# The first block of experts is laid over the attention's early tiles, and token slots carry their row's mean and inverse deviation

## The chip, the cores and the metric

The kernel runs on one core of a Trainium2 chip. Its time is the device time of one execution in microseconds (us), the median of three runs where not said otherwise. The core has five engines with queues of their own: TensorE (PE in the profile; its weight loads are shown apart as PEld), VectorE (DVE), ScalarE (ACT), GpSimd (POOL) and SyncE (SP, which here only issues DMAs). Each works through its queue in order and waits at an instruction until its semaphores are there. Sixteen DMA engines move data for all of them.

## The reference

A tensor `x` of 4 images, 32 by 32 tokens, 384 channels, float32, goes through two layers:

```
x = x + L0_conv(ln(x))      # attention of 12 heads, 1024 tokens an image, with a grouped top-96 mask
t = t + L0_ffn(ln(t))       # 4 experts, the best 2 for each token, 384 -> 1536 -> 384 with gelu
x = x + L1_conv(ln(x))      # outlook attention over 3 by 3 windows
t = t + L1_ffn(ln(t))       # feed-forward whose weights are Kronecker products
```

The part that matters here is the second line. For each token, `ln` takes the mean and the variance of its 384 channels and gives `(v - m) / sqrt(s + 1e-5)`. A gate (384 to 4, then softmax) chooses two experts and their shares; each chosen expert computes `gelu(v @ w1 + b1) @ w2 + b2`; the two answers are added with their shares. The gate needs the same mean and deviation as the experts do.

## The kernel before

**Stages.** `attention` (line 139) runs first, then `experts` (1452), then `outlook` (1596) and `Kron.run` (1936). At the very end stands a general attention behind a run-time test, which these inputs do not enter. On PE, DVE, ACT and SP the instructions of `attention` and `experts` stand in the order in which the Python code issues them. POOL's queue is different: there a planner, which estimates when each instruction will be ready, sets the order when the kernel is built. So a POOL instruction of `experts` can stand among those of `attention`.

**The attention.** There are 48 heads (12 for each image) and four steps a head (`PAIRS`), each with two tiles of 128 keys by 1024 queries. In a step PE makes scores (line 596), ACT the exponentials `e` (606), PE their sums over keys (`total`, 614 into `ps_z`). Once a head has its sums, four small DMAs turn them and spread their reciprocals over the partitions: `z_row` and `zz` (`gather`, 630 and 632), `r_row` and `rz` (`spread`, 644 and 646), all issued by SP. Six steps behind the scores DVE multiplies `e` by `rz` (`share`, 652), and a step later PE multiplies by the values (`out`, 614 into `ps_o`). At the end of a head `keep` copies `ps_o` to the one buffer `po` (672) and adds it up in `q`, by two SP DMAs (681) and two accumulating POOL DMAs (679).

Beside the heads run the preparation of the next image (projections with `wqkv`, transposes into `xnT`, groups with `g`, `gpbd`, `qmbd`), the search for the top 96 (`topk`), the output projection of the image before (`project`), and its routing (`routed`, then `Router.route`), one step of each at a time.

**The routing.** `project` takes the statistics of each finished row with `bn_stats` and `bn_aggr` (722, 723) into `im["mv"]`; `routed` makes the inverse deviation `rs` (742, 752) and the logits; `route` chooses the experts and gives every token two slots in a table in DRAM, of 64 bytes each (`LINE` = 16 words). All 16 words hold the token's number: POOL fills `ids` with an `iota` (1313) and writes it with 16 indirect DMAs (1317), which wait for the slot numbers `there` from DVE (1306). When image 2 of 0 to 3 is routed, `Router.first` (1325) works out the experts and rows of the first four blocks (`NFIRST`), the last of it being `rows_w_first` and `rows_t_first` (1383). Image 3 is routed inside `experts`.

**The end of the attention.** After the last head, DVE and PE make a check over `zall`, `onehot` and `topped` (lines 873 to 887) that sets the flag of the run-time test.

**The experts.** There are 35 blocks of 256 slots. For block n POOL loads by indirect DMA the expert's weights `up` (128 by 4620, 2.37 MB) and `down` (128 by 4992, 2.56 MB; both line 1479), the slots' token numbers `ids` (1490) and the 256 rows of `x1` into `xb` (two DMAs, 1500). `norm` makes the rows' statistics and normalises `xb` in place:

```
nc.vector.bn_stats(st, xb[:, t, :])                                    # 1511, two times
nc.vector.bn_aggr(mv[:, t, :], st)                                     # 1512, two times
nc.scalar.activation(rs, mv[:, :, 1], AF.Sqrt, bias=net.eps["t"])      # 1513
nc.vector.reciprocal(rs, rs)                                           # 1514
nc.vector.tensor_scalar(xb[:, t, :], xb[:, t, :], mv[:, t, 0:1], ...)  # 1516, two times
```

`turn` transposes it into `xbT` (1526, copies 1527). Then PE makes 12 groups of three matmuls into `ps_h` (1568), each followed by a gelu on ACT (1572), and two rows of 12 into `ps_y` (1583), to which DVE adds the bias (1588) and which SP stores (1589). `norm(n + 1)` is issued after the gelus of block n and `turn(n + 1)` before the last row of `ps_y`. Between the gelus of blocks 0 and 1, `beside` puts the projection of image 3 (eight times line 265) and its routing and schedule.

**Memory.** A stage's pools lie on a stack in SBUF and are given back when the stage ends; a tile of the next stage lies where tiles of the last one lay, and its first write waits until those it covers were read for the last time (`reuse_waits="tile"`). Attention and experts begin at the same address. Bytes per partition, from the shapes: `at_const` begins with `wqkv` 13,872, `gpbd` 2,304, `hsel`, `qmbd` 2,304 and holds the check's `topped`, `zall`, `onehot`; `at_big` has `xt` 6,144, `g` 10,240, `xnT` 12,288, three `k` of 4,096, `q4`, `k4`, and `v` 12,288. Over them lie `ex_w1` (two `up` of 18,480), `ex_w2` (two `down` of 19,968), and `ex_blk` (six `ids` of 128, two `xb` and two `xbT` of 3,072). So the first `up` lies over `wqkv`, `gpbd`, `hsel` and most of `qmbd`; the first `down` over the end of `g`, over `xnT` and over two of the `k`; `ids` and `xb` over `v`.

Of the kernel before, what the change touches and what calls it, by code (L numbers as in the profile page):

```python
# [10 lines left out]
FP = mybir.dt.float32  # L11
AF = mybir.ActivationFunctionType
ALU = mybir.AluOpType
# [125 lines left out]
def attention(net, outer, router, x, x1, unsafe, qkv_wT, gpT, proj_wT, proj_w, gate_w, gate_b):  # L139
# [23 lines left out]
    psum = router.psum  # L163
    with ExitStack() as ctx:
        const = ctx.enter_context(tc.tile_pool(name="at_const", bufs=1))
        big = ctx.enter_context(tc.tile_pool(name="at_big", bufs=1))
# [11 lines left out]
        def fetch(b, half, tag="xt"):  # L178
            xt = xts[b, half] = big.tile([P, 4, C], FP, name="xt", tag=tag)
            r = b * NTOK + 512 * half  # L180
            nc.sync.dma_start(out=xt, in_=x[r : r + 512, :].rearrange("(t p) c -> p t c", p=P))

        fetch(0, 0)
        fetch(0, 1, "g")
        wqkv = const.tile([P, KC, 3 * C + NE], FP, name="wqkv")
        for part in range(3):
# [8 lines left out]

        gpbd = const.tile([P, KC, GW], FP, name="gpbd")
        nc.gpsimd.memset(gpbd, 0.0)
# [12 lines left out]
        for t in range(5):  # L210
            for n in range(4):
# [9 lines left out]
                )  # L221
        qmbd = const.tile([P, KC, GW], FP, name="qmbd")
        nc.gpsimd.memset(qmbd, 0.0)
# [17 lines left out]
        def gating():  # L241

            by = big.tile([P, KC, C], FP, name="proj", tag="xt")
            nc.scalar.dma_start(out=by, in_=proj_w.rearrange("(k p) i -> p k i", p=P))
# [181 lines left out]
        def prepare(b):  # L426
# [5 lines left out]
            yield 0, lambda: b == 0 or b - 1 in valued  # L432
            xnT = im["xnT"] = big.tile([P, KC, NTOK], FP, name="xnT", tag="xnT")
            for name in ("col", "inv"):
# [68 lines left out]
        def groups(b):  # L503

            im = images[b]
            for c in range(KC):
                yield 0, lambda: (b, c, "qk") in reached
                q = im["q"][c]

                g = big.tile([P, NB, P + GW], FP, name="g", tag="g")  # L510
                for half in range(2):
# [218 lines left out]
        def routed(b):  # L730
# [23 lines left out]
            nc.vector.tensor_tensor(logit, logit, gate(bgate), ALU.add)  # L754
            yield from router.route(b, logit)
            if b == B - 2:
# [413 lines left out]
class Router:  # L1170
# [67 lines left out]

    def route(self, b, logit):

# [71 lines left out]
        ids = self.temp("ids", [P, NB, self.LINE], mybir.dt.int32)  # L1312
        nc.gpsimd.iota(ids, pattern=[[P, NB], [0, self.LINE]], base=b * NTOK, channel_multiplier=1)
        sent = []
        for t in range(NB):
# [136 lines left out]
def experts(net, router, x1, x2, wup, wdown, beside):  # L1452
# [10 lines left out]
    with ExitStack() as ctx:  # L1463
        def pool(name, bufs, **kw):
            return ctx.enter_context(tc.tile_pool(name=name, bufs=bufs, reuse_waits="tile", **kw))

        wp1, wp2 = pool("ex_w1", 2), pool("ex_w2", 2)
        blk, hp, work = pool("ex_blk", 2), pool("ex_h", 14), pool("ex_work", 4)
        ps_h, ps_y = pool("ex_ps_h", 3, space=PSUM), pool("ex_ps_y", 3, space=PSUM)
# [5 lines left out]
        def weights(n):  # L1475
            up = wp1.tile([P, KC * HID + NF], FP, name="up", tag="up")
            down = wp2.tile([P, NF * C + C], FP, name="down", tag="down")
            for t, w in ((up, wup), (down, wdown)):
                nc.gpsimd.indirect_dma_start(
                    out=t, out_offset=None, in_=w,  # L1480
                    in_offset=bass.IndirectOffsetOnAxis(ap=rows(n)[0], axis=0),
                )
            return up, down
# [4 lines left out]
        def tokens(n):  # L1488
            t = ids[n] = blk.tile([P, TT, router.LINE], I32, name="ids", tag="ids", bufs=6)
            nc.gpsimd.indirect_dma_start(  # L1490
                out=t.rearrange("p t w -> p (t w)"), out_offset=None,
                in_=net.table.rearrange("(r t) w -> r (t w)", t=TT),
                in_offset=bass.IndirectOffsetOnAxis(ap=rows(n)[1], axis=0),
            )

        def fetch(n):
            xb = xbs[n] = blk.tile([P, TT, C], FP, name="xb", tag="xb")
            last = (B - 1 if n < NFIRST else B) * NTOK
# [6 lines left out]
        def norm(n):  # L1505
            xb = xbs[n]
            mv = work.tile([P, TT, 2], FP, name="ln_mv", tag="ln_mv")
            rs = work.tile([P, TT], FP, name="ln_rs", tag="ln_rs")
            for t in range(TT):
                st = work.tile([P, 6], FP, name="ln_st", tag="ln_st")  # L1510
                nc.vector.bn_stats(st, xb[:, t, :])
                nc.vector.bn_aggr(mv[:, t, :], st)
            nc.scalar.activation(rs, mv[:, :, 1], AF.Sqrt, bias=net.eps["t"])  # L1513
            nc.vector.reciprocal(rs, rs)  # L1514
            for t in range(TT):
                nc.vector.tensor_scalar(
                    xb[:, t, :], xb[:, t, :], mv[:, t, 0:1], rs[:, t : t + 1], ALU.subtract, ALU.mult
                )

        def turn(n):  # L1520
            xb = xbs.pop(n)
            xbT = blk.tile([P, KC, XB], FP, name="xbT", tag="xbT")
            for t in range(TT):
# [497 lines left out]
def gates(net, psum, gate_w, gate_b):  # L2021

    tc, nc = net.tc, net.nc
    with ExitStack() as ctx:
# [6 lines left out]
        for b in range(B):  # L2031
            mv, rs = net.ln_stats(range(b * NB, (b + 1) * NB), "t")
            logit = work.tile([P, NB, NE], FP, name="logit", tag="logit")
            for t in range(NB):
# [12 lines left out]
                nc.vector.tensor_tensor(logit[:, t, :], ps[:, :NE], bgate, ALU.add)  # L2047
            yield logit


@with_exitstack
def metaformer_kernel(
# [70 lines left out]
    with tc.If(tc.nc.values_load(unsafe[0:1, 0:1], min_val=0, max_val=1) != 0):  # L2123
        with ExitStack() as outer:
# [4 lines left out]
            with ExitStack() as inner:  # L2129
                router = routing(inner)  # L2130
                for b, logit in enumerate(gates(net, router.psum, gate_w, gate_b)):
                    for _ in router.route(b, logit):
                        pass
# [63 lines left out]
```

## Time and profile before

| what | us |
|---|---|
| median of three runs | 3019.83 (3013.11 to 3023.88) |
| the profiled execution | 3045.37 |
| its span in the profile | 3043.6 |
| attention, to the end of the last `ps_o` matmuls | 0 to 1295.3 |
| from there to block 0's first `ps_h` matmul | 1295.3 to 1321.4 |
| blocks 0 and 1 with projection and routing of image 3 | 1321.4 to 1420.4 |
| blocks 2 to 34 | 1420.4 to 2467.4 |
| outlook and last feed-forward | 2467.4 to 3043.6 |

All but the first row are of one profiled execution, whose own time is 25.5 us above the median of the runs. In the profile's page, part 1 has the busy time of each engine, part 2 the span in 40 slices of 76 us (each digit the busy share in tenths), part 4 the chain of work that ended last, part 5 the groups of like instructions. A line of a group reads: line, engine, operation, output and inputs, shapes, count, then busy time and mean time of one, then how long the engine sat idle before them and what ended it. In answers about a stretch of time, each row begins with the start and the duration in us.

### The profile page before, as it was taken

The page shows a single profiled execution, that of the slowest core. Times are in us where ns is not written, and L with a number is a line of the kernel's source. Part 1 is how long each engine was busy: PE and PEld are TensorE (multiplying, and loading weights), DVE is VectorE, ACT ScalarE, POOL GpSimd, SP SyncE. Part 2 cuts the span into 40 slices and gives each one's busy share as a digit, 9 for nine tenths or more (in the row PEclk, how much of TensorE's full clock was granted, in tenths as well). Part 3 has the DMA queues.
Part 4 walks back from the last instruction along what each step waited for, and adds up shares of the span by engine and source line. Part 5 has one row for each costly group of instructions (what it writes and reads, how often), then busy time and mean ns, then how long its engine had stood idle before and what let it go on. Part 6 is the DMA issues. An engine that isn't in the chain of part 4 may idle for free.

```text
span 3043.6 us, 36874 instructions
## 1 busy us (share of the span) xinstructions
PE 2792.6 (92%) x13236; PEld 1505.7 (49%) x13236; DVE 1398.5 (46%) x3871; ACT 1316.2 (43%) x2130; POOL 390.6 (13%) x496
## 2 busy tenths in 40 slices
PE   6979998899889986668999999999999978999998
PEld 3323343333333431145777777777777744444443
DVE  1467667666766676624111111111111137767652
ACT  3677777677767765312222222222222222212125
POOL 1000000200020002123111112221211012000000
PEclk9999999999999998879999999999999989999999
DMA  5133334222322231254445545555555456544432
GB/s 99 48 92 96 83 95 119 72 53 67 92 53 55 67 97 45 77 202 144 175 178 190 187 177 192 208 211 213 205 195 205 164 167 193 164 147 154 146 120 85
DMA packets 218113, 405.93 MB, mean 133 GB/s; under 512 B 83504, under 2 KB 179296, under 8 KB 204864
## 3 DMA queue, kind: packets, MB, share of 16 engines
q1 hardware_dynamic: 188496, 194.43, 21.5%
q0 software_dynamic: 26432, 206.01, 19.9%
q10 hardware_dynamic: 2992, 3.03, 0.3%
q8 instruction: 107, 1.75, 0.3%
q14 instruction: 86, 0.70, 0.1%
HBM read 305.35 MB, written 49.99 MB: 117 GB/s over the span
## 4 chain that ended last, share of the span: by engine, by line
PE 75%; DVE 7%; ACT 7%; issue 5%; DMA 5%; another core or an unknown queue 1%; POOL 1%; SPq 0%; DVEq 0%; POOLq 0%; ACTq 0%
PE ps_y L1583 17%; PE ps_h L1568 17%; PE ps_t L265 7%; PE ps_z L614 7%; PE ps_s L596 5%; PE ps_o L614 5%; PE ps_a L1693 4%; ACT e L606 4%; PE ps_y L1795 3%; DVE e L652 2%; PE ps_wo L1811 2%; DMA yt<-yg,index 2%; PE ps_v L1737 1%; PE ps_t L399 1%; PE ps_h L1964 1%
## 5 line engine op out<-in xcount | busy, mean ns | idle before, releaser
L1568 PE MATMUL ps_h<-xbT,up 128*128 128x256 f32 x2520 | 555.8, 381 | 2.8 <-ACT h L1572 2.0
L1583 PE MATMUL ps_y<-down,h 128*128 128x384 f32 x1680 | 554.9, 487 | 0.0
L1568 PEld LDWEIGHTS ps_h<-xbT,up 128*128 128x128 f32 x2520 | 481.5, 191 | 78.9 <-ACT h L1572 2.9
L652 DVE CUSTOM_DVE_ANT_0 e<-e,rz,inv 128x1024 f32<-128x1024 f32 x384 | 474.2, 1272 | 60.1 <-DMA rz<-r_row 60.1
L606 ACT ACTIVATE e<-ps_s,shift 128x1024 f32<-128x1024 f32 x384 | 406.5, 1109 | 212.8 <-PE ps_s L596 185.7
L1583 PEld LDWEIGHTS ps_y<-down,h 128*128 128x128 f32 x1680 | 317.5, 191 | 207.2 <-issue 1.7
L614 PE MATMUL ps_z<-e,rt_ones 128*32 128x512 f32 x1536 | 299.0, 635 | 78.2 <-ACT e L606 72.7
L1572 ACT ACTIVATE h<-ps_h,up 128x256 f32<-128x256 f32 x420 | 194.9, 473 | 313.1 <-PE ps_h L1568 308.4
L614 PE MATMUL ps_o<-e,wv 128*32 128x512 f32 x1536 | 279.3, 641 | 22.2 <-DVE wv L659 16.2
L1572 ACT ACT_TABLE_LOAD x37 | 47.5, 1283 | 506.3 <-issue 490.3
L1588 DVE TENSOR_TENSOR y<-ps_y,down 128x384 f32<-128x384 f32 x70 | 39.0, 558 | 413.2 <-PE ps_y L1583 400.4
L596 PE MATMUL ps_s<-q,k 32*128 32x512 f32 x1536 | 221.9, 648 | 0.0
L679 POOL DMA_DIRECT2D q<-po x96 | 75.9, 879 | 1059.3 <-DMA q<-po 604.3
L350 ACT ACTIVATE below<-tk_left,tk_bound 128x1024 bf16<-128x1024 f32 (+1 forms) x160 | 183.9, 1149 | 12.2 <-DVE tk_bound L356 7.6
L1693 PE MATMUL ps_a<-wa,xnT 128*128 128x486 f32 x384 | 171.6, 593 | 12.6 <-DVE attn L1703 12.0
L614 PEld LDWEIGHTS ps_z<-e,rt_ones 128*32 128x32 f32 x1536 | 46.0, 109 | 245.1 <-ACT e L606 198.6
L596 PEld LDWEIGHTS ps_s<-q,k 32*128 32x128 f32 x1536 | 61.2, 186 | 172.6 <-issue 138.3
L1514 DVE RECIPROCAL ln_rs<-ln_rs 128x2 f32<-128x2 f32 x35 | 5.8, 166 | 296.6 <-ACT ln_rs L1513 296.2
L265 PE MATMUL ps_t<-xnT,wqkv 128*128 128x512 f32 x288 | 137.1, 617 | 2.8 <-ACT tk_left L309 1.8
L614 PEld LDWEIGHTS ps_o<-e,wv 128*32 128x32 f32 x1536 | 67.2, 115 | 146.0 <-issue 111.0
L1693 PEld LDWEIGHTS ps_a<-wa,xnT 128*128 128x128 f32 x384 | 72.2, 195 | 98.3 <-issue 89.8
L1795 PE MATMUL ps_y<-band,v 128*32 128x194 f32 (+2 forms) x960 | 108.4, 516 | 4.4 <-DMA band<-room 4.2
(334 smaller groups left out, 3041.2 us busy)
## 6 DMA issues: line engine op xcount, KB each, us to landing
band<-room SPq DMA_DIRECT2D x32, 1560.0 KB
rz<-r_row SPq DMA_DIRECT2D x48, 512.0 KB
yg<-y SPq DMA_DIRECT2D x70, 192.0 KB
q<-q SPq DMA_DIRECT2D x192, 64.0 KB
k<-k SPq DMA_DIRECT2D x192, 64.0 KB
room<-none SPq DMA_DIRECT2D x64, 192.0 KB
x<-x SPq DMA_DIRECT2D x38, 192.0 KB
o<-in_x_dram SPq DMA_DIRECT2D x33, 192.0 KB
```

Source lines behind the costliest of these rows:

```text
L265: nc.tensor.matmul(ps, lhsT=lhsT(k), rhs=rhs(k), start=k == 0, stop=k == KC - 1)
L350: nc.scalar.activation(junk[:n], left[:n], AF.Sign, bias=bound[:n], accum_out=over[:n])
L596: nc.tensor.matmul(ps[:, half * 512 : half * 512 + 512], lhsT=self.k4[r, u * P : (u + 1) * P], rhs=self.q4[r, :], start=True, stop=True,)
L606: nc.scalar.activation(e, ps, AF.Exp, bias=shift, scale=QK_SCALE)
L614: nc.tensor.matmul(ps[r : r + 32, :], lhsT=lhsT(odd), rhs=self.es[2 * u + odd][:, half * 512 : half * 512 + 512], start=u == 0, stop=u == ...
L652: nc.vector.tensor_tensor_reduce(self.es[m], self.es[m], self.rz, 1.0, self.im["inv"][:, m, self.h : self.h + 1], ALU.mult, ALU.add, self. ...
L679: nc.gpsimd.dma_start(out=there, in_=po[r : r + 32, :], accum_op=ALU.add)
L1568: nc.tensor.matmul(ps, lhsT=up[:, o : o + P], rhs=xbT[:, k, :], start=k == 0, stop=k == KC - 1,)
L1572: nc.scalar.activation(h, ps, AF.Gelu, bias=up[:, KC * HID + f : KC * HID + f + 1])
L1583: nc.tensor.matmul(ps, lhsT=hs[f][:, t * P : (t + 1) * P], rhs=down[:, f * C : (f + 1) * C], start=f == 0, stop=f == NF - 1,)
L1693: nc.tensor.matmul(pa[:, hh, :HW_], lhsT=xnT[:, k, :], rhs=wa[:, k, hh * HW_ : (hh + 1) * HW_], start=k == 0, stop=k == KC - 1,)
L1795: nc.tensor.matmul(ys[c][32 * n : 32 * n + 32, lo - 512 * half : hi - 512 * half], lhsT=vs[b, t][:, h * HD : (h + 1) * HD], rhs=bands[b, t ...
```

## The change

It has two parts.

The first part moves tiles. A new pool `at_early` comes first in the attention and holds `wqkv`, `gpbd`, `qmbd`, `xt` (with `proj`), `g` and `xnT`: 13,872 + 2 x 2,304 + 6,144 + 10,240 + 12,288 = 47,152 bytes per partition. In `experts`, the pools `ex_w1`, `ex_w2` and `ex_blk` become two pools `ex_0` and `ex_1`, one for the even and one for the odd blocks, each with one `up`, `down`, `xb` and `xbT`; the six `ids` are in the first. The first pool is 18,480 + 19,968 + 768 + 2 x 3,072 = 45,360 bytes and lies wholly over `at_early`; the second covers the end of `xnT`, `at_const` with the check's tiles, the `k`, `q4`, `k4` and `v`. Buffer counts stay as they were: each kind of tile still has two, used in turn.

The second part moves statistics. `route` gets the mean and the inverse deviation of its rows and copies them, by two DVE copies, into words 1 and 2 of each slot in `ids`, after the `iota` and ahead of the 16 indirect DMAs. `norm` reads them from the block's `ids` as the scalars of its two `tensor_scalar`; its `bn_stats`, `bn_aggr`, `Sqrt` and `reciprocal` are gone. A block's `ids` are therefore read until its `norm`, where before the gather of `xb` was their last reader.

```diff
+        early = ctx.enter_context(tc.tile_pool(name="at_early", bufs=1))
         const = ctx.enter_context(tc.tile_pool(name="at_const", bufs=1))
...
-            xt = xts[b, half] = big.tile([P, 4, C], FP, name="xt", tag=tag)
+            xt = xts[b, half] = early.tile([P, 4, C], FP, name="xt", tag=tag)
...
+        wqkv = early.tile([P, KC, 3 * C + NE], FP, name="wqkv")
+        gpbd, qmbd = (early.tile([P, KC, GW], FP, name=n) for n in ("gpbd", "qmbd"))
         fetch(0, 0)
         fetch(0, 1, "g")
-        wqkv = const.tile([P, KC, 3 * C + NE], FP, name="wqkv")
...
-            xnT = im["xnT"] = big.tile([P, KC, NTOK], FP, name="xnT", tag="xnT")
+            xnT = im["xnT"] = early.tile([P, KC, NTOK], FP, name="xnT", tag="xnT")
...
-                g = big.tile([P, NB, P + GW], FP, name="g", tag="g")
+                g = early.tile([P, NB, P + GW], FP, name="g", tag="g")
...
-            yield from router.route(b, logit)
+            yield from router.route(b, logit, im["mv"][:, :, 0], rs)
...
         nc.gpsimd.iota(ids, pattern=[[P, NB], [0, self.LINE]], base=b * NTOK, channel_multiplier=1)
+        for n, value in enumerate((mean, rs)):
+            nc.vector.tensor_copy(ids.bitcast(FP)[:, :, 1 + n], value)
...
-        wp1, wp2 = pool("ex_w1", 2), pool("ex_w2", 2)
-        blk, hp, work = pool("ex_blk", 2), pool("ex_h", 14), pool("ex_work", 4)
+        halves = [pool(f"ex_{n}", 1) for n in range(2)]
+        hp, work = pool("ex_h", 14), pool("ex_work", 4)
...
-            up = wp1.tile([P, KC * HID + NF], FP, name="up", tag="up")
-            down = wp2.tile([P, NF * C + C], FP, name="down", tag="down")
+            up = halves[n % 2].tile([P, KC * HID + NF], FP, name="up", tag="up")
+            down = halves[n % 2].tile([P, NF * C + C], FP, name="down", tag="down")
...
-            t = ids[n] = blk.tile([P, TT, router.LINE], I32, name="ids", tag="ids", bufs=6)
+            t = ids[n] = halves[0].tile([P, TT, router.LINE], I32, name="ids", tag="ids", bufs=6)
...
-            xb = xbs[n] = blk.tile([P, TT, C], FP, name="xb", tag="xb")
+            xb = xbs[n] = halves[n % 2].tile([P, TT, C], FP, name="xb", tag="xb")
...
             xb = xbs[n]
-            mv = work.tile([P, TT, 2], FP, name="ln_mv", tag="ln_mv")
-            rs = work.tile([P, TT], FP, name="ln_rs", tag="ln_rs")
-            for t in range(TT):
-                st = work.tile([P, 6], FP, name="ln_st", tag="ln_st")
-                nc.vector.bn_stats(st, xb[:, t, :])
-                nc.vector.bn_aggr(mv[:, t, :], st)
-            nc.scalar.activation(rs, mv[:, :, 1], AF.Sqrt, bias=net.eps["t"])
-            nc.vector.reciprocal(rs, rs)
+            own = ids.pop(n).bitcast(FP)
             for t in range(TT):
                 nc.vector.tensor_scalar(
-                    xb[:, t, :], xb[:, t, :], mv[:, t, 0:1], rs[:, t : t + 1], ALU.subtract, ALU.mult
+                    xb[:, t, :], xb[:, t, :], own[:, t, 1:2], own[:, t, 2:3], ALU.subtract, ALU.mult
                 )
...
-            xbT = blk.tile([P, KC, XB], FP, name="xbT", tag="xbT")
+            xbT = halves[n % 2].tile([P, KC, XB], FP, name="xbT", tag="xbT")
```

The path of the general attention, which these inputs do not enter, hands the same two values to `route`.

More of the change, by code (lines that the diff above doesn't have):

```diff
@@ L194, in attention @@
         nc.scalar.dma_start(out=bgate, in_=gate_b.partition_broadcast(P))
-        gpbd = const.tile([P, KC, GW], FP, name="gpbd")
         nc.gpsimd.memset(gpbd, 0.0)
@@ L221, in attention @@
                 )
-        qmbd = const.tile([P, KC, GW], FP, name="qmbd")
         nc.gpsimd.memset(qmbd, 0.0)
@@ L241, in gating @@
         def gating():
-            by = big.tile([P, KC, C], FP, name="proj", tag="xt")
+            by = early.tile([P, KC, C], FP, name="proj", tag="xt")
             nc.scalar.dma_start(out=by, in_=proj_w.rearrange("(k p) i -> p k i", p=P))
@@ L1237, in wide, with route @@
         return pool.tile(shape, FP, name=f"rt_{name}", tag=f"rt_{name}", bufs=1)
-    def route(self, b, logit):
+    def route(self, b, logit, mean, rs):
         nc = self.nc
@@ L2047, in gates @@
                 nc.vector.tensor_tensor(logit[:, t, :], ps[:, :NE], bgate, ALU.add)
-            yield logit
+            yield logit, mv[:, :NB, 0], rs[:, :NB]
 @with_exitstack
@@ L2130, in metaformer_kernel @@
                 router = routing(inner)
-                for b, logit in enumerate(gates(net, router.psum, gate_w, gate_b)):
-                    for _ in router.route(b, logit):
+                for b, given in enumerate(gates(net, router.psum, gate_w, gate_b)):
+                    for _ in router.route(b, *given):
                         pass
```

## The prediction

> **What bounds the kernel now.** I read the page first. In its 40 slices PE is full (9) wherever the experts run, slices 20 to 32, and dips just before, in slices 16 to 18; there the question lies.
>
> ```profile
> span 3043.6 us, 36874 instructions
> ...
> PE   6979998899889986668999999999999978999998
> ...
> DMA  5133334222322231254445545555555456544432
> ```
>
> Then the busy time of each engine by stretch (columns: start and end, length, busy time of PE, PEld, DVE, ACT, POOL, granted PE clock, DMA share, GB/s).
>
> ```profile
> 1295.30:1321.40 26.10, 1.63 (x8) 1.14 (x6) 3.81 (x11) 3.45 (x4) 12.53 (x14) 0.50 0.86 321
> 1425.00:1600.00 175.00, 173.71 (x696) 129.51 (x697) 24.02 (x62) 49.95 (x90) 26.46 (x28) 1.00 0.50 182
> 1600.00:1800.00 200.00, 200.00 (x792) 146.56 (x791) 27.63 (x69) 50.60 (x90) 30.27 (x32) 1.00 0.51 186
> ```
>
> Between attention and experts PE works 1.6 of 26.1 us; from block 2 on it is never free. So the change can be worth something only at the entry and in the routing of image 3, up to 1425. The chain of waits says what the entry waits for:
>
> ```profile
> 1293.33 1.98 PE ps_o L614 x8
> ...
> 1300.42 1.03 POOL up L1479
> ...
> 1305.55 0.94 POOL ids L1490
> ...
> 1306.80 0.95 POOL up L1479
> ...
> 1310.77 5.91 DMA xb<-x,ids
> 1316.71 0.57 DVE ln_st L1511
> ...
> 1318.71 0.49 DVE xb L1516
> ...
> 1319.25 1.55 PE ps_t L1526 x6
> ...
> 1321.44 3.78 PE ps_h L1568 x8
> ```
>
> It is POOL that starts late, then four `ids`, the gather of `xb`, the statistics. POOL's instructions in order of time show where the planner put the loads:
>
> ```profile
> 1285.95 1.81 POOL L1479 DMA_INDIRECT down<-in_wdown_dram,rows_w_first  x1 [0.30 <-DVE s L652]
> 1298.46 1.66 POOL L679 DMA_DIRECT2D q<-po  x2 [10.69 <-DMA q<-po]
> 1300.42 1.03 POOL L1479 DMA_INDIRECT up<-in_wup_dram,rows_w_first  x1 [0.30 <-issue]
> ```
>
> The first `down` stands between the accumulations of the last two heads, so loads can be issued inside the attention. The first `up` stands behind them all, although what it covers was read last at 1223.6 (the matmuls of line 399, with `hsel`). I read this as the planner giving out a pool's ground only when all of it is free: `ex_w1` covered the check's tiles, read until 1294.2.
>
> **The change, part by part.** The sum is made against the profiled execution (3045.37 us: span 3043.6 and 1.8 around it), then taken off the median; that the other runs, 25.5 us shorter, have the same entry is assumed.
>
> *First half over `at_early`.* All of it is read for the last time by 1141.4 (the last copy out of a search's load, line 309); `rows_w_first` is there at 1179.9, `rows_t_first` at 1181.2. The slots must be written before `ids` can be read. Before, image 2's 16 writes ran from 1169.47 to 1192.6, as soon as `there` was cast. Now they wait for the two copies, which stand one routing step later, behind the next `share` (done at 1172.9): I take 4 us, so they end near 1197. Then `up`, `down`, four `ids` and two `xb` are eight issues of 1.25 us, plus a wait of 3.0 for `ids` (as at 1307.75): POOL is through by 1210. The 4.92 MB take 12 us at the 397 to 427 GB/s of the busiest stretches (1290 to 1295, 1305 to 1320). All is there 70 us ahead of need; even behind head 45's accumulation (1265.5) it would be.
>
> What is late next is DVE: the check ends at 1295.75 (1295.61 and 0.14), `norm` is two L1516, and from the first of them to the first `ps_h` before took 1321.44 - 1318.71 = 2.73. So block 0 starts at 1298.5 in place of 1321.4: **-23.0 us**. `up` and `down` of block 1 still wait for the check and go at about 1300; they land within 21 us (the first `up`: issued 1300.42, used 1321.44), and block 1 starts 45.5 us after block 0. Cover enough. The last head's L679 feeds the first projection, six gelus in (near 1309), 9 us after its issue.
>
> *No statistics, blocks 1 and 3 to 34.* Removed for each: two L1511 of 0.53, two L1512 of 0.18, one L1514 of 0.17 on DVE; on ACT a `Sqrt` of 0.30, its table load and the load back to gelu. In blocks 2 to 34 nothing of it is on the path: PE waited 2.0 us for ACT in all, the last column of
>
> ```profile
> L1568 PE MATMUL ps_h<-xbT,up 128*128 128x256 f32 x2358 | 514.4, 379 | 2.0 <-ACT h L1572 2.0
> L1513 ACT ACT_TABLE_LOAD x32 | 41.1, 1283 | 0.6
> ```
>
> PE's own work covers them; without that cover they would cost about 3 us a block. Taken: 0. The Trainium skill disagrees on its face: "ScalarE: Activation LUTs", section "What ACT_TABLE_LOAD costs", prices each switch of table set at about 2.66 us with its drain. By that page 69 fewer loads would give 184 us; the row shows three `ps_h` buffers hiding them.
>
> *No statistics, block 2.* Here DVE is the path: routing and schedule keep it busy from 1380 to 1406.8 without a gap, `norm(2)` stands behind, and PE waits 6.8 us for it until 1409.44. From 1406.82 to 1408.81 is statistics: 1.99 saved, less image 3's two copies, each like the COPY of line 1281 (0.17): **-1.65**. Right after, at 1424.64, PE waits 1.65 for a gelu behind a table load that is gone; DVE waited for PE until the same moment, so it may stay. Between 0 and -1.65: **-0.8**.
>
> *Copies of images 0 to 2.* Six of 0.17 = 1.0 us on DVE, which is 7% of the whole chain but most of it in routing steps: between 0 and +1.0, **+0.5**. They wait for POOL's `iota`, done long before (image 3's at 1194.9). Image 3's writes start up to 0.75 later on POOL; `tokens(4)` behind them feeds a block 50 us away: 0. `ids` held until `norm` delay only loads six blocks ahead: 0.
>
> *The weight stream under the attention.* From about 1198 to 1211 it meets the row DMAs. Head 44's four were issued at 1209.88 (`z_row`), 1211.59, 1213.69 and 1215.13 (`rz`, landing 1219.1); DVE already waited 2.5 us for `rz`. Nearest row: an `xb` gather took 5.91 beside the weights (1310.77) and about 3.9 without (1448.14 to 1452.0), 2.0 more. Four links make 8.2 if all are hit, 0 if the stream is over: **+2**, as only the first link or two fall into it. A rule speaks against the change here: "DMA: Bandwidth & Descriptors", section "Queues, rings and completion order", says that each DMA engine takes turns between queue rows with work, packet by packet. By it a link would up to double (1.7, 1.7, 1.4 and 3.6 make 8.4), the sum would be 16 and not 23.
>
> *Outlook.* The planner orders that stage anew. Its first POOL instructions lay over the last `down` and waited until 2468.0; now they lie over the odd half. The first gathers can go 3.2 us earlier (2470.68 against 2467.5), but the first PE work waits for `x` (landed 2476.1), which did not move. Between -3.2 and +3.2 (another order): 0.
>
> Sum: -23.0 - 1.65 - 0.8 + 0.5 + 2 = -22.9. The profiled execution would take 3022.5, the median **2997**. With all bounds 2990 to 3008.
>
> **The rivals.** *The load stays late* (the change doesn't do what it says): the planner keeps `up` behind the last L679. Then only the statistics go, 1316.71 to 1318.71, with block 2's: 2.0 + 1.65 + 0.8, so 3015. For it: the first `up` did stand there. Against: its pool covered the check, the new one does not, and `down` was let through.
>
> *Weights early, `xb` late.* If `ids` or `xb` slip behind the last L679, `xb` is issued at 1300.4, lands by 1306.3 and block 0 starts 3 us later: gain near 14, 3006. Against: nothing that `xb` covers is read after `xnT`.
>
> *POOL's queue blocks* (slower). If the planner sets a load that isn't ready ahead of a head's L679, that L679 waits, `po` is not free, ACT's copy 672 and then PE's `ps_o` are late. Between L679 of head 42 (ended 1204.5) and the next copy (1220.5) lie 16 us of slack. A wait of W costs W - 16 and the gain is 22.9: from W = 39 it loses, at 60 the time is 3041. For it: POOL already sat 26.8 us ahead of the slots' first write. Against: rows and ground are free by 1181, both before head 42's accumulation.
>
> **How the numbers follow.** The sum's case 0.74 (its own range 2987 to 3010, the bounds and some 3 us for the median's spread), `xb` late 0.10, load late 0.06, POOL blocked 0.07, another order of the outlook or attention at 10 us or more 0.03. 0.3% is 9 us, about what a measurement here can tell from no change. Faster: 0.74, 0.10 and a little of the last, 0.85; same 0.07; slower 0.08. The range 2985 to 3013 holds the first two but for their tails, and leaves out the others.
>
> **What the changed profile would show.** The first `up` and `down` in POOL's queue near 1198, before head 43's L679; two L1516-like instructions right behind the check; PE's gap after the last `ps_o` near 3 us; no `Sqrt` in blocks 0 to 34; blocks still 31.7 us each; `norm(2)` about 2 us shorter before `turn(2)`; `rz` of head 44 landing up to 8 us late. Wrong would make me: `up` behind the check, a stretched head near 1210, or an outlook that is not 460 us to its last band.

## The result, and the profile after

The changed kernel took **3006.0 us** (median of 22 runs, 2996.7 to 3014.4) against 3016.4 for the kernel before (22 runs, 3010.8 to 3023.9): a ratio of 0.9967, with a 95% interval of 0.9960 to 0.9975. It is faster by 10.4 us, or 0.33%; forecast were 22.9.

The change does at the entry what the forecast said. The chain of waits of the changed kernel, from the last `ps_o` to block 1 (start, length, work):

```profile
1279.94 0.85 PE ps_o L615 x4
1281.23 0.49 DVE xb L1516
1281.77 1.55 PE ps_t L1526 x6
1283.34 0.57 DVE xbT L1527
1283.96 11.75 PE ps_h L1568 x42
...
1298.28 6.28 DMA x<-o
1304.64 2.53 DMA o<-in_x_dram
...
1313.68 9.64 DMA o<-in_x_dram
...
1324.73 0.47 DVE xb L1516
1325.34 0.91 PE ps_t L1526 x6
1326.25 9.43 PE ps_y L1583 x24
1335.68 1.29 PE ps_h L1568 x6
```

From the last `ps_o` (ended 1280.80) to the first `ps_h` are 3.2 us in place of 26.1, and no statistics stand between. New is what follows: the chain leaves PE and runs over the projections' residues, a store of `x` that takes 6.28 us and a load of `o` that takes 9.64.

POOL's instructions show the other half of the forecast, and its flaw (start, busy time, instruction, idle time before and its releaser):

```profile
1178.77 0.99 POOL L1486 DMA_INDIRECT up<-in_wup_dram,rows_w_first  x1 [0.30 <-PE ps_o L615]
1180.07 1.06 POOL L1486 DMA_INDIRECT down<-in_wdown_dram,rows_w_first  x1 [0.30 <-issue]
1181.43 2.80 POOL L1497 DMA_INDIRECT ids<-table,rows_t_first  x1 [0.30 <-issue]
...
1195.28 0.95 POOL L1507 DMA_INDIRECT xb<-x,ids  x1 [7.00 <-DMA ids<-table,rows_t_first]
```

`up` and `down` do go 100 us ahead of need. But the next row link of a head is issued 4.9 us later, into their stream. SP's queue of the changed kernel there:

```profile
1183.69 0.54 SPq L631 DMA_DIRECT2D z_row<-zr  x1
1189.63 0.37 SPq L633 DMA_DIRECT2D zz<-z_row  x1
1196.09 0.33 SPq L645 DMA_DIRECT2D r_row<-rr  x1
1198.48 0.32 SPq L647 DMA_DIRECT2D rz<-r_row  x1
```

Each link waits for the one before it. `z_row` takes 5.9 us until `zz` can be issued, and `zz` 6.5 until `r_row`. DVE, which waits for `zz` in the middle of its queue, has the last `share` of head 43 behind it, so PE's last `ps_o` of head 43 starts only at 1199.01. Then the copy of `po` waits once more. PE, POOL and ACT of the changed kernel, and the same copy in e2 (below), which has no early stream:

```profile
1199.01 1.93 PE L615 MATMUL ps_o<-e,wv 128*32 128x512 f32 x8 [5.58 <-DVE topped L390]
1198.03 1.81 POOL L680 DMA_DIRECT2D q<-po  x2
1205.77 0.59 ACT L673 COPY po<-ps_o 128x512 f32<-128x512 f32 x1 [13.45 <-DMA k<-k]
1192.03 0.59 ACT L672 COPY po<-ps_o 128x512 f32<-128x512 f32 x1 [2.01 <-PE ps_o L614]
```

There is one buffer `po`, and head 42's accumulation (L680), which has to read it, stands in POOL's queue behind the two gathers of `xb`, the first of which waits 7.0 us for `ids`. The second of these accumulating DMAs landed at 1205.63 (the last update of its semaphore, for which ACT's queue waits there; the row names a load of `k`), 0.14 us ahead of the copy. So the copy of head 43's `po` comes 32.2 us after that of head 42: `ps_o` is some 6.7 us late by the links, and the copy 4.8 us later by POOL's queue.

**Stages.** The first profile of before took 3045 us and has long waits in the attention. A third chip, on which e8 to e11 ran, shows the same waits and takes 3044.7 us for this kernel; the two chips of e1 to e7 took 3015. It is called the slower chip here, the other two the faster ones. On which chip the first profile was taken is not on record; by its waits it belongs to the slower one, and the profile of the changed kernel, which has none of them, to the faster ones. The fair pair is two profiles from the slower chip, e8 (before) and e9 (changed). The ends of the stages are the last `ps_o`, the first `ps_h` of blocks 0, 1 and 2, and the last `ps_y`, all read on PE's timeline, in us:

| stage | before (e8) | changed (e9) | difference | forecast |
|---|---|---|---|---|
| to the last `ps_o` | 1293.2 | 1304.7 | +11.5 | +2.5 |
| entry | 25.8 | 3.2 | -22.7 | -23.0 |
| block 0 | 45.6 | 51.9 | +6.3 | 0 |
| block 1, with image 3's routing | 53.4 | 51.2 | -2.1 | -1.65 |
| blocks 2 to 34 | 1047.0 | 1045.1 | -2.0 | -0.8 |
| outlook | 577.2 | 575.6 | -1.6 | 0 |
| span | 3042.2 | 3031.7 | -10.5 | -22.9 |

Two stages gave back 17.8 us of a gain of 28.4. The first of them is not the stream's alone: the copy of head 41's `po`, ahead of any early load, already comes 4.6 us later in e9 than in e8. Up to there the profiles differ by several us whatever the edit (on the faster chips the copy of head 42 falls between 1168.3 and 1175.8), so what the stream costs is read from the heads behind it.

### The profile page after: what moved, and what is told of

Read it like the earlier page. It is cut to its first block, busy times and chain, and to the rows that moved or that the text cites. A ratio compares the mean times of both kernels' runs of the same rounds, so it can differ in the third digit from the quotient of the medians.

```text
span 3006.7 us, 36661 instructions
## 1 busy us (share of the span) xinstructions
PE 2793.6 (93%) x13236; PEld 1509.9 (50%) x13236; DVE 1344.4 (45%) x3704; ACT 1222.3 (41%) x2026; POOL 396.4 (13%) x496
## 4 chain that ended last, share of the span: by engine, by line
PE 78%; ACT 7%; DVE 6%; DMA 5%; issue 4%; POOL 0%; SPq 0%; DVEq 0%; POOLq 0%; ACTq 0%
PE ps_h L1568 18%; PE ps_y L1583 17%; PE ps_t L266 7%; PE ps_z L615 7%; PE ps_s L597 6%; PE ps_o L615 5%; PE ps_a L1693 4%; ACT e L607 4%; PE ps_y L1795 3%; DVE e L653 2%; PE ps_wo L1811 2%; DMA yt<-yg,index 2%; PE ps_v L1737 1%; PE ps_h L1964 1%; PE ps_t L400 1%
## 5 line engine op out<-in xcount | busy, mean ns | idle before, releaser
L680 POOL DMA_DIRECT2D q<-po x96 | 75.7, 874 | 1058.2 <-DMA q<-po 622.2
L1693 PE MATMUL ps_a<-wa,xnT 128*128 128x486 f32 x384 | 172.2, 595 | 10.7 <-DVE attn L1703 10.0
L615 PEld LDWEIGHTS ps_z<-e,rt_ones 128*32 128x32 f32 x1536 | 45.6, 109 | 228.4 <-ACT e L607 190.0
L1538 DVE SCALAR_TENSOR_TENSOR x<-yt,weight,x 128x384 f32<-128x384 f32 x38 | 23.5, 619 | 191.9 <-DMA x<-x 191.3
L1507 POOL DMA_INDIRECT xb<-x,ids x70 | 66.9, 955 | 251.4 <-PE ps_t L1526 218.4
```

The lines of the kernel that those rows point to most:

```text
L615: nc.tensor.matmul(ps[r : r + 32, :], lhsT=lhsT(odd), rhs=self.es[2 * u + odd][:, half * 512 : half * 512 + 512], start=u == 0, stop=u == ...
L680: nc.gpsimd.dma_start(out=there, in_=po[r : r + 32, :], accum_op=ALU.add)
L1693: nc.tensor.matmul(pa[:, hh, :HW_], lhsT=xnT[:, k, :], rhs=wa[:, k, hh * HW_ : (hh + 1) * HW_], start=k == 0, stop=k == KC - 1,)
```

## The experiments

The cuts of code are shortened to what matters. "Heads 43 and 44" is the time from the copy of `po` of head 42 to that of head 44. The expectations count the row link at 1183.69 as head 43's; by the code it is head 44's, whose links stall head 43's last `share`.

**The two parts alone.** e1 keeps the two halves, puts the statistics back into `norm` and takes the two copies out of `route`:

```
     def norm(n):
-        own = ids.pop(n).bitcast(FP)
+        mv, rs = bn_stats, bn_aggr, Sqrt and reciprocal of xb, as before
     # in route, behind the iota:
-    nc.vector.tensor_copy(ids.bitcast(FP)[:, :, 1 + n], value)
```

> Only the memory part of the change: the two halves, the first over the early tiles; the slots stay as before and every block makes its statistics. From the changed kernel's profile I now hold that its first half brought 22.9 us at the entry and lost about 11.4 in the attention (the weights meet the row transfers of head 43) and 6.0 in block 0 (residues). Here the entry keeps 2.0 us of statistics, norm(2) another 1.65 to 2, the gelu wait 1.65: about 5 us slower than the whole change, so near 3011, 5 us faster than before; PE's gap after the last ps_o near 5 us. By the recorded prediction, without the two collisions, it would be 3016 - 18.5, near 2998. If the switches of ACT's table are not hidden but paid at the 2.66 us each that the Trainium skill gives (ScalarE: Activation LUTs, What ACT_TABLE_LOAD costs), it is over 150 us slower than the whole change.

Measured: 3000.8 us, ratio 0.9947 (0.9930 to 0.9963), 14 us faster than before and not 5. Entry 5.3 us and block 1 53.3 us are 2 us each more than in the changed kernel, as expected; but block 0 took 45.6 and heads 43 and 44 took 49.0 us, against 51.6 and 53.4. In this kernel the weights left 9.3 us ahead of `z_row`, not 4.9. On the slower chip (e10, below) the same kernel's block 0 took 51.8 us, so escaping the residues' stall was this execution's timing and no property of e1: here the last packet of block 1's weights ended 0.5 us after the first store was issued, in e10 3.4 us and in the changed kernel 4.7 us after.

e1 settles the statistics of the other 33 blocks. It makes 72 loads of ACT's table in the blocks (the changed kernel 3), and PE does not notice. The groups of e1 (busy time, mean ns | idle time before):

```profile
L1518 ACT ACT_TABLE_LOAD x35 | 44.9, 1283 | 0.6
L1573 PE MATMUL ps_h<-xbT,up 128*128 128x256 f32 x2520 | 555.7, 382 | 0.8 <-DVE xbT L1532 0.7
```

and the same group of the changed kernel:

```profile
L1568 PE MATMUL ps_h<-xbT,up 128*128 128x256 f32 x2520 | 556.8, 382 | 0.8 <-DVE xbT L1527 0.7
```

Blocks 2 to 34 take 1044.86 us with the statistics and without them. The Trainium skill ("ScalarE: Activation LUTs", "What ACT_TABLE_LOAD costs") has the load itself right, 1283 ns; its 2.66 us for a switch is a price of ACT's time, and 69 of them, an estimated 184 us, cost this kernel nothing there. On the slower chip they cost one wait: PE stands 1.8 to 2.0 us for a gelu early in block 2 in all four profiles with statistics (the first one, e8, e10, e11), and not in e9.

e2 is the other part on the kernel before: the slots carry the two numbers, the memory stays.

```
-    mv, rs = statistics of xb
+    own = ids.pop(n).bitcast(FP)
     # in route, behind the iota:
+    nc.vector.tensor_copy(ids.bitcast(FP)[:, :, 1 + n], value)
```

> Only the other part: mean and inverse deviation ride in the slots, the blocks make no statistics, memory and so the late load stay as before. Saved on the path: 2.0 us at the entry, 1.65 to 2 at norm(2), 1.65 at the gelu of block 2, less 0.5 of copies: near 3011.5, 4 to 5 us faster than before. If the 35 normalisations were on the path (3 us each) it would be near 2910; if the table switches cost 2.66 us each, near 2830. The blocks from 2 on should last 31.7 us as before.

Measured: 3012.4 us, ratio 0.9993 (0.9981 to 1.0004): 2.7 us less than before, not told from nothing. Its stages say what was expected: entry 24.6, block 1 50.3 (PE's wait ahead of `turn(2)` fell from 6.8 to 4.3), blocks 2 to 34 1044.9. It also gives what the attention is without an early stream on the faster chips: last `ps_o` at 1266.6, heads 43 and 44 in 41.6 us. SP's queue of e2 at the links that the changed kernel stretched:

```profile
1181.38 0.53 SPq L630 DMA_DIRECT2D z_row<-zr  x1
1183.09 0.37 SPq L632 DMA_DIRECT2D zz<-z_row  x1
1185.19 0.33 SPq L644 DMA_DIRECT2D r_row<-rr  x1
1186.63 0.32 SPq L646 DMA_DIRECT2D rz<-r_row  x1
```

1.7, 2.1 and 1.4 us, and `rz` was used at 1190.87: 9.5 us from `z_row` on. In the changed kernel it was used at 1205.17, 21.5 us.

**The stream under the attention.** e4 holds `up` and `down` of block 0 each until the `rz` of a head has landed, so that each falls in the pause ahead of the next `z_row`:

```
 in Head.share, behind the first product with rz (m == 0):
+    if self.n == 44: hold(0)      # self.n == 45: hold(1)
 def hold(self, i):
+    nc.vector.tensor_copy(w[:, NFIRST + i : NFIRST + i + 1], w[:, 0:1])
 weights(0):
-    by rows_w_first[:, 0:1] for both
+    up by the first copy, down by the second
```

> The changed kernel with block 0's up and down each held by a copy of its row of indices that DVE makes right behind the first share of head 44 (up) and of head 45 (down), so that each 2.4 MB goes in the pause between one head's rz and the next head's z_row, and not in one stream of 12 us over head 43's links. If that stream is what costs the attention 11.4 us (z_row 5.9 us, zz 8.9 us of wait, rz 6.2), most of it comes back: near 2996, copies of po 43 back to some 21 us after 42. If the attention's loss is from the new places of its tiles or from the slot copies, it stays near 3006. If each held half still meets links, it lies between, near 3001.

Measured: 2997.4 us, ratio 0.9938 (0.9922 to 0.9955). POOL's queue of e4, and SP's at head 45's links:

```profile
1198.85 1.25 POOL L1495 DMA_INDIRECT up<-in_wup_dram,rows_w_first  x1 [6.93 <-DVE rows_w_first L1451]
1219.37 1.82 POOL L1495 DMA_INDIRECT down<-in_wdown_dram,rows_w_first  x1 [17.07 <-DVE rows_w_first L1451]
```

```profile
1206.73 0.54 SPq L632 DMA_DIRECT2D z_row<-zr  x1
1209.38 0.37 SPq L634 DMA_DIRECT2D zz<-z_row  x1
1212.26 0.33 SPq L646 DMA_DIRECT2D r_row<-rr  x1
1213.67 0.32 SPq L648 DMA_DIRECT2D rz<-r_row  x1
```

The end of `up` still touches `z_row` (2.7 us) and `zz` (2.9), which the head's slack covers: heads 43 and 44 take 41.6 us, as with no early stream. POOL's first `xb` waits 0.2 us here and not 7.0, and head 42's accumulation lands 3.0 us ahead of the copy. The same bytes, moved, cost nothing there; so on the faster chips it is the place of the stream that cost the 11.8 us (53.4 - 41.6), by the links and by POOL's queue.

e5 moves the stream in another way: `iota` and the two copies are made one routing step earlier, so that the table writes, and the weights behind them, need not wait for the copies.

```
     nc.scalar.activation(prob, prob, AF.Exp)
     yield
+    ids = ...; iota; two copies       # before: after the last yield of route
```

> The changed kernel with iota and the two copies into the slots made one routing step after the start of an image's routing (behind the Exp) in place of right ahead of the writes. In the changed kernel image 2's first table write waits 4.5 us for the copies (DVE's cast at 1150.23, the write at 1155.69; without copies, e1_halves, 1147.04 and 1147.99), the weights behind the 16 writes go that much later, and come 4.9 us ahead of head 43's z_row in place of 9.3. If it is this distance that made the attention 4.4 us worse than e1_halves (heads 43 and 44 together 53.4 us against 49.0; without a stream, e2_slots, 41.6), the two heads take about 49 us here and the time is near 3001.5. If the copies cost by themselves or not at all, it stays near 3006.

Its profile fits: weights 8.3 us ahead of `z_row`, heads 43 and 44 in 49.2 us. With the other profiles of the faster chips this is a series: 4.9 us ahead cost 11.8, 6.9 (e3) 11.0, 8.3 (e5) 7.6, 9.3 (e1) 7.4. But the median is 3005.2, ratio 0.9965 (0.9954 to 0.9977), not told from the changed kernel's; the profiled execution was the fastest of eleven (2998.0 to 3010.3). The series is shown for single executions, the gain in the median is not.

**The residues.** In the changed kernel the projections of image 3 get their residues through two buffers: add, store, and only then the load into the same buffer. e3 gives each of the seven late ones a buffer and issues them together:

```
 def left(pool):
-    for t in range(NB):
-        if t + 1 < NB: residue(B - 1, t + 1)
+    for t in range(1, NB): residue(B - 1, t, pool)     # tag "o_late", bufs=NB - 1
+    for t in range(NB):
         project(B - 1, t)
```

> The changed kernel with the seven residue loads of image 3's projections issued together into seven buffers, ahead of block 1's weights, in place of two buffers that each wait for a store. If the wait of 3.7 us ahead of turn(1), and the slow clock after it (24 ps_y in 9.43 us against 7.74 before), come from residue loads and stores that share the queues' engines with block 1's weights, block 0 gets 5 to 6 us shorter: near 3000.5, block 1's first ps_h some 46 us after block 0's. If DVE's queue or the projections themselves set it, nothing changes: 3006.

Measured: 3002.8 us, ratio 0.9956 (0.9938 to 0.9973), an interval that overlaps the changed kernel's; the gain shows in the stage: block 0 took 46.4 us, as expected. DVE's waits between block 0's start and `turn(1)` (total, times, longest), in the changed kernel:

```profile
DVE o L720 <- DMA o<-in_x_dram: 17.0, 4, 8.8
DVE o L720 <- PE ps_t L266: 15.7, 2, 13.8
```

and in e3:

```profile
DVE o L723 <- PE ps_t L266: 23.7, 6, 14.3
```

DVE waits for PE alone, and the loop is no longer the chain. From the first store to the issue of the load behind it 6.4 us pass in the changed kernel, 7.3 in e4, 6.6 in e5 and 6.5 in e9, beside block 1's weights issued 8 to 11 us before; in e8 it is 1.9, with the weights long there:

```profile
1333.02 0.33 SPq L724 DMA_DIRECT2D x<-o  x1
1334.95 0.33 SPq L701 DMA_DIRECT2D o<-in_x_dram  x1
```

A loop that is 3 us late then sends the load for its sixth projection just behind block 2's `up` (1312.74, when block 0's last gelu has freed the ground), and that load takes the 9.64 us. PE stands for 3.7 us, and the next 24 `ps_y` run 9.43 us in place of 7.74, at a granted clock of 0.81 (mean from 1326 to 1335) in place of 1.00.

The control, the same edit on the kernel before:

> Control: the kernel before with the residues loaded first and nothing else. There the weights of block 1 have landed when the projections run, block 0 took 45.5 us and DVE waited for no residue. If the gain of e3 comes from the collision alone, nothing changes here: 3015, block 0 near 45.5. If loading residues early helps by itself (fewer stores waited for), it is 4 to 5 us faster: 3010.5.

It was slower: 3021.8 us, ratio 1.0019 (1.0004 to 1.0033). The chain of waits of e7 at the entry:

```profile
1270.36 8.64 DMA o<-in_x_dram
...
1279.05 8.37 DMA xb<-x,ids
```

The residue loads now move with the late weights of block 0, and `xb`, which took 5.9 us there before, takes 8.4; the entry grew to 28.5 us, from 25.8 to 26.2 in the two profiles of before. So loading early has no worth of its own: it pays where it gets out of the way of a stream, and costs where it gets into it. The entry accounts for some 2.5 of the 6.9 us; the rest of that difference is not explained (the profile is of the fastest of ten runs).

**Both cures.**

> Both cures together on the changed kernel: up and down of block 0 held to the pauses behind the rz of heads 44 and 45, and the seven residues loaded first. If the two losses are separate (11.8 us in heads 43 and 44, 4 to 6 us in block 0), the gains add up: block 0 near 46.4 us, heads 43 and 44 near 41.6, the time near 2993, some 23 us faster than before. If the residues' gain depends on the late weights, it stays at e4_hold's 2997.

Measured: **2988.0 us, ratio 0.9911 (0.9894 to 0.9927)**, 27 us faster than before, the best of all. The edit is that of e3 and e4 together. The entry takes 3.2 us and block 0 46.6; PE's gaps from there to block 2 are the 4.7 us of the routing and 4.1 ahead of `turn(2)`. Heads 43 and 44 took 45.3 us in its profile, better than 53.4 but not the 41.6 expected. The median is 5 us better than expected all the same; of the profile, the outlook took 572.5 us, some 3 less than in every other but e10 (572.8), which nothing here explains.

Of the 3.7 us that were missing in the heads, 2.6 are POOL's queue by itself: the links take about as long as in e4 (10.9 us from `z_row` to the use of `rz`, 10.7 there), `ps_o` is in time, and the copy of head 43's `po` waits for head 42's accumulation, which stands behind `ids` and `xb` (the other 1.1 us fall in head 44, just behind):

```profile
1187.26 1.81 POOL L683 DMA_DIRECT2D q<-po  x2
1193.15 0.59 ACT L676 COPY po<-ps_o 128x512 f32<-128x512 f32 x1 [4.58 <-DMA k<-k]
```

All profiles of the faster chips with `ids` and `xb` loaded under the attention, and e2, in us ("landed" is the last semaphore update of head 42's second accumulation):

| run | weights ahead of `z_row` | `z_row` to use of `rz` | last `ps_o` of head 43 ends | landed | copy of head 43 | heads 43 and 44 |
|---|---|---|---|---|---|---|
| e2 | no early stream | 9.5 | 1191.98 | 1181.98 | 1192.03 | 41.6 |
| changed | 4.9 | 21.5 | 1200.94 | 1205.63 | 1205.77 | 53.4 |
| e3 | 6.9 | 19.8 | 1199.64 | 1204.16 | 1204.31 | 52.6 |
| e5 | 8.3 | 16.9 | 1192.48 | 1196.34 | 1196.48 | 49.2 |
| e1 | 9.3 | 16.2 | 1194.01 | 1198.02 | 1198.16 | 49.0 |
| e4 | held | 10.7 | 1196.51 | 1193.60 | 1196.56 | 41.6 |
| e6 | held | 10.9 | 1190.53 | 1193.01 | 1193.15 | 45.3 |

In all five with a loss the copy starts 0.14 to 0.15 us after the accumulation has landed. A kernel in which that accumulation goes ahead of `ids` and `xb` was not run; since `rz` of the changed kernel is used only at 1205.17, it should give back little by itself there.

**On the slower chip.** The last four runs ask whether the first profile's long waits belong to the kernel, and compare the parts side by side: e8 is the kernel before, e9 the changed one, e10 the kernel of e1, and e11 that of e1 with the edits of e3 and e4.

> A second profile of the kernel before, unchanged. The first took 3045 us, 29 over the median, with waits of 8 to 9 us ahead of the accumulations of heads 18, 30 and 42 that no other profile here has. If these are accidents of that one execution, the last ps_o ends near 1267 (e2_slots: 1266.6), heads 43 and 44 take 41.6 us together, the stretch behind the last ps_o is again near 1746 to 1748 us. If the kernel before has them always, it ends near 1295 again.

> The changed kernel once more, on the same chip as e10, to compare the two. 3006, some 10 us faster than before; heads 43 and 44 together 50 us or more, block 0 50 to 52 us.

> The memory part alone once more. By its stages it should beat the whole change: heads 43 and 44 take 49.0 us in place of 53.4 and block 0 45.6 in place of 51.6, against 2.1 more at the entry and 2.1 more in block 1: 6 us faster than e9. If the difference in the medians of e1 (3000.8) was chance, and statistics are what counts, it is 4 us slower than e9.

> The memory part with held weights and residues first, statistics still made in every block: e6 without the slots. With no collision left for the slots to shift, taking out the statistics should be worth what its stages say, 2.1 us at the entry and 2 to 3 in block 1: so this kernel about 4.5 us slower than e6's 2988, near 2992.5. If the statistics are worth nothing, 2988; if the slots cost in themselves, faster than 2988.

Before took 3044.7 us on this chip (19 runs), the changed kernel 3033.0 (ratio 0.9961, 0.9945 to 0.9978), e10 3029.5 (0.9952, 0.9934 to 0.9970), e11 3020.5 (0.9923, 0.9904 to 0.9942). Three things follow.

- The long waits of the first profile are neither an accident of one execution nor a property of the kernel: they are back in e8 (last `ps_o` at 1293.2) and in e9 to e11, and absent from all profiles of the faster chips.
- e10 against e9 does not show that the halves alone beat the whole change; the intervals overlap, in e1 too. Nor does it show the 4 us that the statistics should be worth. The likely reason is that each early stream falls where it falls: e10 took 6.2 us from its first store to the load behind it, and its block 0 51.8.
- With the stream held and the residues first, e11 has 76.0 us from the copy of head 41 to that of head 44, as e8 has, against 83.2 in e9; its block 0 takes 45.8. But its copy of head 41 comes 8.5 us later than in e8, ahead of the stream and unexplained. Its ratio and that of e6, 0.9923 and 0.9911, differ by 3.6 us in the direction and about the size of the statistics at entry and block 1 (4.5 expected), but their intervals overlap.

## Why the prediction was right and wrong

The time, 3006.0, lies inside the stated 2985 to 3013, and 9 us above the forecast median of 2997. That is in part luck: the gain was 10.4 us and not 22.9, because the stream left its bounds and block 0 lost 6 us for which the sum had no term. The range had room for that because its bounds also held the outlook's order and `xb` late.

- **Entry, -23.0: right**, 22.7 to 23.0, by the mechanism named: the first pool's ground free early, the check next on the path.
- **"The weight stream under the attention ... +2, as only the first link or two fall into it": this step failed most.** It cost 11.8 us on the faster chips, outside its own bounds of 0 to 8.2: 6.7 by the links up to head 43's `ps_o`, most of the rest by POOL's queue (next point). The place was wrong: the forecast read 12 us between the weights (1198) and head 44's `z_row` (1209.88) off a profile in which ACT stood idle for 7.3 us from 1186.9 on; that held back the heads, but not POOL's writes and what follows them, and the runs on the faster chips, which were to be forecast, have no such wait. Without it 4.7 are left, and 4.9 were measured. The price was wrong too: a link was priced by a gather that lost 2.0 us beside the weights; `z_row` lost 4.2 and `zz` 4.4. The estimate made from the rule of the Trainium skill that was weighed against it, turns between queues ("DMA: Bandwidth & Descriptors", "Queues, rings and completion order"), was nearer with its 8.4 for four links, and still too small: the four lost 12.0. It took a turn of each queue as equally long, which the packets of this case are not (last section).
- **"POOL's queue blocks", priced at a loss only from a wait of 39 us: it came true in small.** A gather that was not ready (`xb`, 7.0 us for `ids`, where the sum had 3.0) stood ahead of head 42's accumulation, and `po` was not free, as that rival says. The accumulation was issued 24.5 us after its copy in place of 7.2 (e2) and took 7.0 us to land in place of 2.9; so the slack, 16 us by the forecast and 10.0 from its landing to the next copy in e2, was used up, and the next copy waited 4.8 us. "Rows and ground are free by 1181" was true and not enough: the gather waits for `ids`, too.
- **"Cover enough": the second failure.** It asked whether block 1's weights come in time. They do. It did not ask what else moves at that time: the two-buffer loop of stores and residue loads, which used to run after them. That is +6.0 to 6.3 us in block 0, priced at nothing.
- **No statistics in blocks 3 to 34, 0: right**, shown by e1 to 0.01 us. PE's wait for the gelu, -0.8: it went away on the slower chip (-2.0 in blocks 2 to 34) and was never there on the faster ones. `norm(2)`, -1.65: PE's wait ahead of `turn(2)` fell by 3.0 in the profile (2.5 in e2), block 1 by 2.1.
- **Copies, +0.5 on DVE: the cost was named at the wrong place.** As forecast ("I take 4 us") they delay the table writes, by 4.5 us; that mattered through the stream behind the writes.
- **Outlook, 0: measured -1.2 to -1.6**, inside its bounds, and less than it varies between profiles (572.5 us in e6, 576.9 in e11).
- On the slower chip the loss in the attention is as large, 11.5 us, but only 7.1 of it lie between heads 41 and 44 and 4.6 ahead of them. Between them ACT waited longer (5.5, 6.5 and 1.7 us, releasers unnamed) while `z_row` was issued 20.7 us behind the weights. Holding the stream removes the 7.1 (e11); how the stream caused them on that chip is not settled.

The other rivals did not come true. Two collisions cost the forecast's own case 17.8 us, where its sum had 2 for the one and nothing for the other; the other stages were some 3 us better than forecast.

## What to carry to other kernels

A load that is started earlier moves its bytes through somebody else's time: list every transfer on a chain of waits that is in flight then, the small ones first, and place the load in their pauses, if need be by a copy of its index that is made when the pause begins. Look, too, at what stands behind it in the queue that issues it: an instruction that frees a single buffer must not stand behind a gather that waits. A loop of load, add and store through two buffers had no slack to lose here; when a bulk load moves next to it, give it its buffers. And a distance in time between two queues is only as good as the waits between them: before building on it, look whether a wait there is one that the runs to be forecast have.

## What the runs showed of the hardware

- A small transfer beside a bulk one took over three times as long here. While the changed kernel's `z_row` of 8 KB was under way (1183.7 to 1189.6), the DMA view shows these shares of the 16 engines:

```profile
DMA packets 152, 2.45 MB, mean 416 GB/s; under 512 B 20, under 2 KB 20, under 8 KB 24
## 3 DMA queue, kind: packets, MB, share of 16 engines
q0 software_dynamic: 143, 2.43, 96.9%
q8 instruction: 1, 0.02, 1.0%
q1 hardware_dynamic: 8, 0.01, 0.4%
```

  The packets themselves show that it waits: 127 of the 143 carry weights, 18 or 20 KB each, and take 0.7 us each (median); `z_row` is four packets of 2 KB, and four of 4 bytes that follow. Each of the 2 KB takes about 0.1 us, as in e2. But the first of them starts 3.8 us after the issue (1.2 in e2), and from there to the end of the last of the eight 1.8 us pass (0.2 in e2). So the link takes 5.9 us in place of 1.7. That the size of the weights' packets is what makes these waits so long was not tried.
- Two chips ran the kernel before in 3015 us and a third in 3044.7. Most of it is three waits, at heads 18, 30 and 42, where the intervals between copies of `po` are 30.4, 37.8 and 34.4 us in e8 against 23.1, 29.6 and 26.1 in e2. ACT's waits in e8 around the last of them:

```profile
ACT e L606 <- remote: 7.4, 1, 7.4
ACT e L606 <- PE ps_s L596: 4.9, 3, 2.6
```

  "remote" is a releaser that the records of this core don't name; e2 has no such line. What it is was not found.
